# Macaron transformer block: a rearranged first feed-forward stage

## The chip, the cores and the metric

The kernel runs on one core of a Trainium2 chip. The core has five engines with an instruction stream each: TensorE (PE, matrix products), VectorE (DVE, element-wise work and reductions), ScalarE (ACT, activations and copies), GpSimd (POOL, element-wise work) and SyncE (SP, here only DMA issues). Every engine executes its own stream in order; semaphores hold an instruction until its inputs are there. Data lies in an on-chip memory of 128 partitions (SBUF); products go to banks of a second memory, PSUM, from which DVE and ACT read. The metric is the time of one execution on the device in microseconds (us).

## The reference

The input is x, 4 sequences of 1024 rows of 512 numbers. The block is

```python
x = x + 0.5 * ffn(layernorm(x), w_gate_up, w_proj)
x = x + attention(layernorm(x), Wq, bq, Wk, bk, Wv, bv, Wo, bo)
x = x + 0.5 * ffn(layernorm(x), w_gate_up, w_proj)

def ternary_quant(w_fp32, g=64):
    w = w_fp32.astype(bfloat16)
    w_g = w.reshape(-1, g)
    scale = clip(mean(abs(w_g), -1, keepdims=True), 1e-08, None)
    q = clip(round(w_g / scale), -1, 1)
    w_hat = (q * scale).reshape(w.shape)
    return w + (w_hat - w)

def ffn(x, w_gate_up, w_proj):          # w_gate_up: 4096 x 512, w_proj: 512 x 2048
    gate, up = split(x @ ternary_quant(w_gate_up).T, 2)
    h = silu(gate) * up                 # 2048 wide
    h = h * rsqrt(mean(h * h, -1) + eps)
    return h @ ternary_quant(w_proj).T
```

The attention has 32 query heads and 8 key heads of 16 numbers, with a rotary position code. All products work in float32 precision; in the feed-forward each activation is cut into a rounded high part and the low rest, and both are multiplied with the weight.

## The kernel before

The rows are worked in blocks of 512 (two per sequence). The kernel runs one long chain of stages. The first stage, class `First`, does the feed-forward for the two blocks of sequence 0 and at the same time prepares all feed-forward weights, because they arrive as float32 and must be quantized and transposed. Later stages (`FeedForward`, label "0" to "4") do the feed-forward of the other blocks with the prepared weights, and attention stages lie between. What follows the first stage is not touched by the change.

The hidden width of 2048 is cut into 16 weight groups hc of 128. A group has three parts of 128 x 512 numbers: part 0 gate, part 1 up, part 2 the projection. What a group goes through, with the lines of the kernel before:

- `load` (L415): three DMAs on SP bring the parts as float32 into a tile `w` of 128 x 1536, of which there is one.
- `cast` (L429): ACT rounds them to bfloat16 (`wb`, three buffers).
- `double` (L439): ACT makes twice the absolute value (`twice`, two buffers).
- `scales` (L447): DVE reduces absolute values over 64 columns (L455), makes the scale (L457); `widen` (L462) then lets ACT spread each scale over its 64 columns (`wide`, one buffer).
- `signs` (L470): DVE compares `twice` with `wide` for a mask (L482), takes the sign bit of `wb` (L484) and ORs it with the scale (L485) into `wq` (one buffer).
- `quantize` (L489): DVE subtracts, adds and multiplies with the mask (L494 to L496), as the reference rounds.
- `transpose` (L498): PE transposes each part (L503). ACT copies parts 0 and 1 to SBUF as `guT` (L511) and part 2 as `w_pT` (L505), which stays for the whole kernel. For the later stages POOL casts each `guT` to bfloat16 (`g16`, L513), and SP stores it to DRAM in `d_guT` (L514).

For block k (0 or 1) and group hc the products run thus:

- `product` (L542): for part 0 or 1, four 128-wide chunks of the input, each with the high part `xT` and the low part `xL`: eight matmuls into one PSUM bank with the tag "gu" (L546). After part 0, ACT takes the Silu into `sg` (L555). `start` does both parts.
- `finish` (L563): DVE multiplies Silu(gate) with up: h (L575). Block 1's h are all kept.
- `halves` (L578): ACT rounds h to `high` (L584); then DVE or POOL subtracts for `low` (L585). `tally` (L589): the square of h is added to a running sum `acc` on POOL (L603); for block 0 POOL also makes the square (the function passed in at L662).
- `project` (L237): eight matmuls with `w_pT` (L245) add to four output banks "po". There are four "gu" and four "po" banks, and block 1 can be projected only after block 0's outputs have left theirs.
- `factors` and `end` (L267, L280): PE sums `acc` over the partitions (L258), DVE and POOL make the inverse root, and DVE adds the scaled output to x (L288, four times).

`begin_groups` (L609) is the lead: it loads x, normalizes block 0 (`normal_scales` L100, `normalize` L174, with `turned` L124 for the transposes, ACT's copy to `xT` L131 and DVE's subtraction for `xL` L133), and brings group 0 through its parts. `group(i)`, for i from 0 to 17, is the steady part. In the kernel before block 1 lags block 0 by two groups: group i projects block 0's group i-2, transposes group i, does `start(1, i-2)` and later `start(0, i)`, and on the way quantizes group i+1, reduces the scales of group i+2 and casts group i+3. Block 1's rows are normalized in groups 0 and 1. In the groups 5 to 15 attention weights are loaded, transposed and stored on the side (`attention_weights` L518), and x tiles of the next sequence are loaded. `projection` (L386) follows: it splits block 1's kept h and projects them.

The order is written by hand: within `manual_schedule` each engine's stream takes its instructions in the order of the program. Two such parts that follow one another may be interleaved (the trace has the next stage's weight copies, L94, among the last groups). The order of one group on DVE and ACT is set by these lines:

```python
                steps = self.scales(i + 2)
                self.start(1, i - 2)
                self.signs(i + 1)
...
            self.cast(i + 3)
            self.load(i + 4)
            self.double(i + 2)
            for widen in steps:
                widen()
            if i >= 2:
                self.finish(1, i - 2)
            if 2 <= i < HC:
                self.start(0, i)
            if i >= 2:
                self.quantize(i + 1)
```

Of the kernel before, what the change touches and what calls it, by code (L numbers as in the profile page):

```python
# [37 lines left out]
def tile_macaron_block(  # L38
# [58 lines left out]
    def inverse_root(dst, src, n):  # L97
        nc.gpsimd.tensor_tensor(dst, src, mhalf[:, :n], ALU.pow)

    def normal_scales(tiles, label):  # L100

        n = len(tiles)
        mv = small.tile([P, n, 2], F32, tag="mv", name=f"mv_{label}")
        for i, t in enumerate(tiles):
            st = small.tile([P, 6], F32, tag="st", name=f"st_{label}_{i}")
            nc.vector.bn_stats(st, t)
            nc.vector.bn_aggr(mv[:, i, :], st)
        var = small.tile([P, n], F32, tag="var", name=f"var_{label}")
        nc.vector.tensor_scalar(var, mv[:, :, 1], LN_EPS, None, ALU.add)
        rstd = small.tile([P, n], F32, tag="rstd", name=f"rstd_{label}")  # L110
        inverse_root(rstd, var, n)
        return mv, rstd
# [243 lines left out]
    class First(FeedForward):  # L356
# [7 lines left out]
        def groups(self):  # L364

            self.kept = tc.tile_pool(name="kept", bufs=1)
            self.banks = tc.tile_pool(name="fp0a", bufs=4, space=PSUM)
            self.keep, self.ps = self.kept.__enter__(), self.banks.__enter__()
            self.w, self.wb, self.wide, self.twice, self.q = {}, {}, {}, {}, {}
            self.sg, self.made, self.units, self.parts = {}, {}, {}, {}  # L370
            self.turns, self.turning = [], []

            for n in range(4):
                self.pos.setdefault(0, []).append(
                    self.ps.tile([P, D], F32, tag="po", name=f"po_0a_0_{n}")
                )
            with tc.tile_pool(name="f0a", bufs=1) as wp, tc.tile_pool(name="wstage", bufs=1) as stage:
                self.wp, self.stage = wp, stage
                self.ident16 = stage.tile([P, P], BF16, tag="ident16", name="ident16")
                nc.vector.tensor_copy(self.ident16, ident)  # L380
                with tc.manual_schedule():
                    self.begin_groups()
                    for i in range(HC + 2):
                        self.group(i)

        def projection(self):  # L386
# [25 lines left out]

        ALL = ((0, 12),)

        def load(self, hc):  # L415
            if hc >= HC:
                return
            w = self.stage.tile([P, 12, P], F32, tag="w", name=f"w_{hc}")
            r = slice(hc * P, (hc + 1) * P)
            ru = slice(H + hc * P, H + (hc + 1) * P)  # L420
            nc.sync.dma_start(w[:, 0:4, :], w_gate_up[r, :].rearrange("p (c k) -> p c k", k=P))
            nc.sync.dma_start(w[:, 4:8, :], w_gate_up[ru, :].rearrange("p (c k) -> p c k", k=P))
            nc.sync.dma_start(w[:, 8:12, :], w_proj[:, r].rearrange("(c p) k -> p c k", p=P))
            self.w[hc] = w

        def sixteen(self, name, hc, bufs=1):
            return self.stage.tile([P, 12 * P], BF16, tag=name, name=f"{name}_{hc}", bufs=bufs)

        def cast(self, hc, some=ALL):  # L429
            if hc < HC:  # L430
                if hc not in self.wb:
                    self.wb[hc] = self.sixteen("wb", hc, 3)
                for a, z in some:
                    nc.scalar.copy(
                        self.wb[hc][:, a * P : z * P],
                        self.w[hc][:, a:z, :].rearrange("p c k -> p (c k)"),
                    )

        def double(self, hc, some=ALL):  # L439
            if hc < HC:  # L440
# [57 lines left out]
        def transpose(self, hc, part):  # L498
# [5 lines left out]
            if part == 2:  # L504
                nc.scalar.copy(w_pT[hc].rearrange("p (c k) -> p c k", k=P), pt)  # L505
                return
            name = f"guT_{hc}_{part}"
            w = (widened.tile if part else self.stage.tile)(
                [P, DC, P], F32R, tag="guT", name=name, bufs=3
            )  # L510
            nc.scalar.copy(w, pt)  # L511
            w16 = narrow_tile(f"g16_{hc}_{part}")
            nc.gpsimd.tensor_copy(w16, w.bitcast(F32))  # L513
            nc.sync.dma_start(d_guT[hc, part], w16.rearrange("p c k -> p (c k)"))  # L514
            for k in range(2):
                self.weights.setdefault((k, hc), []).append(w)

        def attention_weights(self, n):  # L518

# [21 lines left out]

        def product(self, k, hc, part):  # L542
            pg = self.ps.tile([P, 512], F32, tag="gu", name=f"gu_0a_{k}_{hc}_{part}")
            for c in range(DC):
                for low, xp in enumerate(self.inputs[k]):
                    nc.tensor.matmul(  # L546
                        pg,
                        lhsT=self.weights[k, hc][part][:, c, :],
# [2 lines left out]
                        stop=(c == DC - 1 and low == 1),  # L551
                    )
            if part == 0:
                sg = self.sg[k, hc] = self.wp.tile([P, 512], F32, tag="sg", name=f"sg_0a_{k}_{hc}")
                nc.scalar.activation(sg, pg, AF.Silu)  # L555
            else:
                self.made[k, hc] = pg
# [50 lines left out]

        def begin_groups(self):  # L609

            thirds = [((a, a + 4),) for a in (0, 4, 8)]
            for i in range(4):
                load_x(0, i)
            self.load(0)
            for i in range(4, NT):
                load_x(0, i)
            for third in thirds:
                self.cast(0, third)
            self.load(1)
            self.double(0, thirds[0])  # L620
            scales = normal_scales(self.tiles(0), "0a_0")
            for widen in self.scales(0, thirds[0]):
                widen()
            turns = list(self.normalize(0, range(4), self.wp, self.ps, "gu", 4, scales))
            self.signs(0, thirds[0])
            self.quantize(0, thirds[0])
            for turn in turns:
                turn()
            steps = self.scales(0, thirds[1])
            self.double(0, thirds[1])  # L630
            steps[0]()
            self.transpose(0, 0)
            self.product(0, 0, 0)
            self.signs(0, thirds[1])
            self.quantize(0, thirds[1])
            steps = self.scales(0, thirds[2])
            self.double(0, thirds[2])
            steps[0]()
            self.transpose(0, 1)
            self.cast(1)  # L640
            self.load(2)
            self.double(1)
            self.product(0, 0, 1)
            self.signs(0, thirds[2])
            self.quantize(0, thirds[2])
            self.transpose(0, 2)
            self.cast(2)
            self.load(3)
            for widen in self.scales(1):
                widen()  # L650

        def group(self, i):
            self.finish(0, i - 1)
            if 2 <= i:
                for some in ([0, 1], [2, 3]):
                    self.project(0, i - 2, self.parts[0, i - 2][0], some)
            if i == HC + 1:
                self.end(0, self.factors(0))
            if 1 <= i <= HC:
                self.halves(0, i - 1, nc.gpsimd)  # L660
                self.parts[0, i - 1][1]()
                self.tally(0, i - 1, lambda dst, h: nc.gpsimd.tensor_tensor(dst, h, h, ALU.mult))  # L662
            if 1 <= i < HC:
                for part in range(3):
                    self.transpose(i, part)
            if i < 2:
                if i > 0:
                    self.start(0, i)
                some = [2 * i, 2 * i + 1]
                self.signs(i + 1)  # L670
                self.quantize(i + 1)
                steps = self.scales(i + 2)
                scales = normal_scales(self.tiles(1, some), f"0a_1_{i}")
                rows = list(self.normalize(1, some, self.wp, self.ps, "gu", 4, scales))
                for turn in self.turning:
                    turn()
                self.turning = rows
            else:
                for turn in self.turning:
                    turn()  # L680
                self.turning = []
                steps = self.scales(i + 2)
                self.start(1, i - 2)
                self.signs(i + 1)
            if 5 <= i < 15:
                self.turns.append(self.attention_weights(i - 5))
            self.cast(i + 3)
            self.load(i + 4)
            self.double(i + 2)
            for widen in steps:  # L690
                widen()
            if i >= 2:
                self.finish(1, i - 2)
            if 2 <= i < HC:
                self.start(0, i)
            if i >= 2:
                self.quantize(i + 1)
            if 6 <= i < 16:
                self.turns.pop(0)()
            if 2 <= i < 2 + NT:  # L700
                load_x(1, i - 2)
# [771 lines left out]
```

## Time and profile before

| | before |
|---|---|
| median of 3 runs | 3166.78 us (3166.61 to 3167.30) |
| profiled execution | 3165.26 us, span 3163.5 us |
| PE busy | 3089.3 us (98%), mean granted clock 0.991 |
| DVE / ACT / POOL busy | 2177.3 / 1757.6 / 915.2 us |
| first block-0 product (L546) | 17.94 us |
| 0 to 60 us, PE busy | 25 of 60 us, clock 0.91, 0.50, 0.67 in thirds |
| transposes of the steady groups (L503) | at 104.65, 115.27, 125.91, 136.53 us |
| 100 to 180 us, of each 20: PE, DVE, ACT, POOL | 19.3 to 20.0, 19.7, 13.6 to 15.2, 11.6 to 11.9 |
| first matmul of block 1's projection (L245) | 220.48 us |

Times of single instructions are microseconds from the start of the span. A row in order of time has the start, the length, the engine, the line, the operation, output and inputs with their shapes, how many equal ones were merged, and in brackets how long the engine had been idle before and what released it. A row of a stretch has its bounds, its length and the busy time of PE, PE's weight loads, DVE, ACT and POOL (instructions in brackets), the clock granted to PE, the share of DMA and GB/s. Matmuls are pipelined, so each is listed longer than the distance to the next, and ends on PE are modelled.

### The profile page before, as it was taken

The page shows a single profiled execution, that of the slowest core. Times are in us where ns is not written, and L with a number is a line of the kernel's source. Part 1 is how long each engine was busy: PE and PEld are TensorE (multiplying, and loading weights), DVE is VectorE, ACT ScalarE, POOL GpSimd, SP SyncE. Part 2 cuts the span into 40 slices and gives each one's busy share as a digit, 9 for nine tenths or more (in the row PEclk, how much of TensorE's full clock was granted, in tenths as well). Part 3 has the DMA queues.
Part 4 walks back from the last instruction along what each step waited for, and adds up shares of the span by engine and source line. Part 5 has one row for each costly group of instructions (what it writes and reads, how often), then busy time and mean ns, then how long its engine had stood idle before and what let it go on. Part 6 is the DMA issues. An engine that isn't in the chain of part 4 may idle for free. (4 is left out here: it accounts for less than half of the span.)

```text
span 3163.5 us, 46228 instructions
## 1 busy us (share of the span) xinstructions
PE 3089.3 (98%) x16896; PEld 1953.4 (62%) x16896; DVE 2177.3 (69%) x3656; ACT 1757.6 (56%) x2346; POOL 915.2 (29%) x865
## 2 busy tenths in 40 slices
PE   5999999999999999999999999999999999999999
PEld 4777777733358777533387777333587776333787
DVE  7977666588846665788666665888556666887343
ACT  5752333389953333699913333899523335999343
POOL 2564333300034343200053333000243432000344
PEclk7999999999999999999999999999999999999999
DMA  3443322224334133143242222243341231342111
GB/s 110 156 136 97 92 62 80 60 87 107 115 89 127 55 94 109 48 125 95 89 121 85 88 81 62 76 111 117 88 131 56 77 97 62 94 126 66 40 60 41
DMA packets 231267, 285.52 MB, mean 90 GB/s; under 512 B 30048, under 2 KB 176736, under 8 KB 231040
## 3 DMA queue, kind: packets, MB, share of 16 engines
q1 hardware_dynamic: 224448, 272.32, 29.1%
q0 software_dynamic: 6592, 10.24, 1.4%
q8 instruction: 134, 2.20, 0.3%
q14 instruction: 93, 0.76, 0.1%
HBM read 215.35 MB, written 66.45 MB: 89 GB/s over the span
## 5 line engine op out<-in xcount | busy, mean ns | idle before, releaser
L1171 DVE TENSOR_REDUCE pm<-sm 128x1 f32<-128x512 f32 x2048 | 1281.8, 684 | 207.8 <-PE sm L1162 202.0
L1302 ACT ACTIVATE e<-s 128x1024 f32<-128x1024 f32 x1024 | 990.7, 1023 | 124.9 <-PE s L1293 121.7
L205 PE MATMUL gu<-xT,guT 128*128 128x512 f32 x1792 | 706.9, 394 | 4.3 <-DVE ql L1088 2.8
L205 PE MATMUL gu<-xL,guT 128*128 128x512 f32 x1792 | 700.8, 391 | 0.7 <-DVE xL L133 0.7
L1309 PE MATMUL o<-e,vs 128*32 128x512 f32 x4096 | 548.2, 604 | 0.0
L1162 PE MATMUL sm<-p_m,p_m 64*128 64x512 f32 x2048 | 491.9, 411 | 5.9 <-DVE h L217 5.9
L1293 PEld LDWEIGHTS s<-p_s,p_s 64*128 64x128 f32 x2048 | 193.8, 183 | 483.7 <-ACT e L1302 466.0
L1293 PE MATMUL s<-p_s,p_s 64*128 64x512 f32 x2048 | 467.7, 451 | 8.8 <-ACT e L1302 8.7
L225 POOL TENSOR_TENSOR sq<-h 128x512 f32<-128x512 f32 x210 | 218.7, 1042 | 713.9 <-DVE h L217 713.9
L217 DVE TENSOR_TENSOR h<-sg,gu 128x512 f32<-128x512 f32 x224 | 153.8, 686 | 375.4 <-PE gu L205 361.6
L215 ACT ACTIVATE sg<-gu 128x512 f32<-128x512 f32 x224 | 134.2, 599 | 479.5 <-PE gu L205 479.5
L205 PEld LDWEIGHTS gu<-xT,guT 128*128 128x128 f32 x1792 | 337.8, 188 | 78.8 <-ACT guT L94 3.2
L205 PEld LDWEIGHTS gu<-xL,guT 128*128 128x128 f32 x1792 | 337.8, 188 | 71.9 <-DVE xL L133 1.3
L245 PE MATMUL po<-w_pT,high 128*128 128x512 f32 x896 | 374.2, 418 | 0.9 <-DVE x L288 0.9
L245 PE MATMUL po<-w_pT,low 128*128 128x512 f32 x896 | 355.0, 396 | 0.0
L231 ACT CAST high<-h 128x512 fp32r<-128x512 f32 x224 | 139.0, 621 | 327.0 <-DVE h L217 320.6
L1162 PEld LDWEIGHTS sm<-p_m,p_m 64*128 64x128 f32 x2048 | 229.6, 185 | 83.3 <-DVE h L217 50.2
L229 POOL TENSOR_TENSOR acc<-acc,sq 128x512 f32<-128x512 f32 x205 | 275.9, 1346 | 16.1
L94 ACT CAST guT<-g 128x512 fp32r<-128x512 bf16 x448 | 274.9, 614 | 7.9 <-ACT guT L94 5.5
L245 PEld LDWEIGHTS po<-w_pT,high 128*128 128x128 f32 x896 | 168.2, 188 | 94.3 <-issue 56.4
L1309 PEld LDWEIGHTS o<-e,vs 128*32 128x32 f32 x4096 | 81.1, 108 | 183.3 <-issue 156.0
L233 DVE TENSOR_TENSOR low<-h,high 128x512 fp32r<-128x512 f32 x224 | 169.1, 755 | 35.4 <-ACT high L231 35.4
(159 smaller groups left out, 2869.3 us busy)
## 6 DMA issues: line engine op xcount, KB each, us to landing
g<-d_guT SPq DMA_DIRECT2D x448, 128.0 KB
p_m<-d_q SPq DMA_DIRECT2D x56, 512.0 KB
p_s<-d_q SPq DMA_DIRECT2D x56, 512.0 KB
d_o<-oT SPq DMA_DIRECT2D x64, 256.0 KB
p_m<-d_km SPq DMA_DIRECT2D x56, 256.0 KB
p_s<-d_ks SPq DMA_DIRECT2D x56, 256.0 KB
x<-in_L_attn_x_dram SPq DMA_DIRECT2D x32, 256.0 KB
w<-in_L_ffn_w_gate_up_dram SPq DMA_DIRECT2D x32, 256.0 KB
```

Of the source, the lines that this page charges most:

```text
L94: nc.scalar.copy(w, t)
L205: nc.tensor.matmul(pg, lhsT=self.weights[k, hc][part][:, c, :], rhs=xp[:, c, :], start=(c == 0 and low == 0), stop=(c == DC - 1 and low == 1),
L217: nc.vector.tensor_tensor(h, sg, gu[1], ALU.mult)
L225: nc.gpsimd.tensor_tensor(sq, h, h, ALU.mult)
L229: nc.gpsimd.tensor_tensor(acc, acc, sq, ALU.add)
L233: return (high, low), lambda: nc.vector.tensor_tensor(low, h, high.bitcast(F32), ALU.subtract)
L245: nc.tensor.matmul(self.pos[k][i], lhsT=h[:, i * P : (i + 1) * P], rhs=w_pT[hc], start=(hc == 0 and n == 0), stop=(hc == HC - 1 and n == 1),)
L1162: nc.tensor.matmul(s, lhsT=q[j // 2][at, i * P : (i + 1) * P], rhs=k[at, half * 512 : (half + 1) * 512], start=True, stop=True,)
L1171: nc.vector.tensor_reduce(pm[:, i, j, half : half + 1], s, AX.X, ALU.max)
L1293: nc.tensor.matmul(s[:, e, :], lhsT=lhsT[at], rhs=rhs[at, queries], start=(kc == 0 and n == 0), stop=(n == len(terms) - 1), skip_group_che ...
L1302: return w, lambda: nc.scalar.activation(w, s, AF.Exp, scale=1.0 / HD**0.5)
L1309: nc.tensor.matmul(o[j * SLOT : (j + 1) * SLOT, :], lhsT=vs[:, kc, g, :], rhs=es[j // 2][:, j % 2, :], start=(kc == 0), stop=(kc == NT - 1),)
```

## The change

Block 1 no longer lags. In each group both blocks' products of that weight group are made, block 0's first. The rows of block 1 are normalized in the lead, and the lead brings groups 0 and 1 through both blocks' products; `group` then runs from i = 2.

Inside a group the order is new: transposes first, then h of block 1's last group, `halves` and `tally` of block 0's last group, the projection of block 0's group i-2, signs of group i+1, cast and double of group i+2, block 0's products, quantize of group i+1, the narrow copies, scales and widening of group i+2, h of block 0, block 1's products.

Weights are loaded in thirds into four buffers of 128 x 512; each cast of a third issues the load of the third four further on. `wb` and the part-0 `guT` have two buffers instead of three, and `sg` two instead of one. The narrow copies (`g16`) are made by ACT in `narrow_ones`, a step of its own, instead of by POOL in `transpose`. A product takes its four high matmuls first and then the four low ones. An activation on a single column at the start makes ACT load the table with Silu early. The end of the loop changes with it: block 0's last projection and sums now come after all products.

```diff
-    def normal_scales(tiles, label):
+    def normal_scales(tiles, label, between=lambda i: None):
...
             nc.vector.bn_aggr(mv[:, i, :], st)
+            between(i)
...
-                    for i in range(HC + 2):
+                    for i in range(2, HC + 2):
                         self.group(i)
...
+        def load(self, upto):
+            while self.loaded < min(upto, 3 * HC):
+                hc, part = divmod(self.loaded, 3)
+                w = self.stage.tile([P, DC, P], F32, tag="w", name=f"w_{hc}_{part}", bufs=4)
...
+                nc.sync.dma_start(w, src)
+                self.w[hc, part] = w
+                self.loaded += 1
...
+        def cast(self, hc, parts=range(3)):
             if hc < HC:
                 if hc not in self.wb:
-                    self.wb[hc] = self.sixteen("wb", hc, 3)
+                    self.wb[hc] = self.sixteen("wb", hc, 2)
+                for part in parts:
                     nc.scalar.copy(
+                        self.wb[hc][:, part * 512 : (part + 1) * 512],
+                        self.w.pop((hc, part)).rearrange("p c k -> p (c k)"),
                     )
+                    self.load(3 * hc + part + 5)
...
             nc.scalar.copy(w, pt)
-            w16 = narrow_tile(f"g16_{hc}_{part}")
-            nc.gpsimd.tensor_copy(w16, w.bitcast(F32))
-            nc.sync.dma_start(d_guT[hc, part], w16.rearrange("p c k -> p (c k)"))
+            self.wide_ones.append((hc, part, w))
...
+        def narrow_ones(self):
+            for hc, part, w in self.wide_ones:
+                w16 = narrow_tile(f"g16_{hc}_{part}")
+                nc.scalar.copy(w16, w.bitcast(F32))
+                nc.sync.dma_start(d_guT[hc, part], w16.rearrange("p c k -> p (c k)"))
+            self.wide_ones = []
...
-            for c in range(DC):
-                for low, xp in enumerate(self.inputs[k]):
+            for low, xp in enumerate(self.inputs[k]):
+                for c in range(DC):
...
         def begin_groups(self):
...
+            warm = self.stage.tile([P, 1], F32, tag="warm", name="warm")
+            nc.scalar.activation(warm, ones, AF.Silu)
+            load_x(0, 0)
+            load_x(0, 1)
+            self.load(1)
+            load_x(0, 2)
+            load_x(0, 3)
+            self.load(3)
             for i in range(4, NT):
                 load_x(0, i)
+            self.load(4)
+            normal = normal_scales(self.tiles(0), "0a_0", first_third)
+            self.double(0, b)
+            scales(0, b)
+            turns = list(self.normalize(0, range(4), self.wp, self.ps, "gu", 4, normal))
+            quantized(0, a)
             for turn in turns:
                 turn()
             self.transpose(0, 0)
             self.product(0, 0, 0)
+            quantized(0, b)
             self.transpose(0, 1)
+            self.cast(0, [2])
             self.product(0, 0, 1)
+            normal = normal_scales(self.tiles(1), "0a_1")
+            self.double(0, c)
+            scales(0, c)
+            turns = list(self.normalize(1, range(4), self.wp, self.ps, "gu", 4, normal))
+            self.finish(0, 0)
+            for turn in turns:
+                turn()
+            self.cast(1, [0])
+            self.double(1, a)
+            self.product(1, 0, 0)
+            self.product(1, 0, 1)
+            quantized(0, c)
+            scales(1, a)
             self.transpose(0, 2)
+            self.cast(1, [1, 2])
+            quantized(1, a)
+            rest = ((4, 12),)
+            self.double(1, rest)
+            scales(1, rest)
+            self.transpose(1, 0)
+            self.finish(1, 0)
+            self.product(0, 1, 0)
+            quantized(1, rest)
+            self.transpose(1, 1)
+            self.narrow_ones()
             self.cast(2)
+            self.double(2)
+            self.product(1, 1, 0)
+            self.transpose(1, 2)
+            scales(2, self.ALL)
+            self.product(0, 1, 1)
+            self.finish(0, 1)
+            self.halves_of(0)
+            self.product(1, 1, 1)
+            quantized(2, self.ALL)
+            self.cast(3)
+            self.double(3)
+            scales(3, self.ALL)
 
         def group(self, i):
+            if i < HC:
+                for part in range(3):
+                    self.transpose(i, part)
+            self.finish(1, i - 1)
+            if i <= HC:
+                self.halves_of(i - 1)
+            for some in ([0, 1], [2, 3]):
+                self.project(0, i - 2, self.parts[0, i - 2][0], some)
             if i == HC + 1:
                 self.end(0, self.factors(0))
+                return
+            self.signs(i + 1)
+            if i < HC:
+                self.cast(i + 2)
+                self.double(i + 2)
+                self.start(0, i)
+            self.quantize(i + 1)
+            self.narrow_ones()
+            steps = self.scales(i + 2)
+            for widen in steps:
+                widen()
+            if i < HC:
+                self.finish(0, i)
+                self.start(1, i)
             if 5 <= i < 15:
                 self.turns.append(self.attention_weights(i - 5))
             if 6 <= i < 16:
                 self.turns.pop(0)()
             if 2 <= i < 2 + NT:
                 load_x(1, i - 2)
```

Here `first_third` casts, doubles and scales the first third of group 0 after the second x tile's statistics and casts the second third; `quantized` is signs and quantize together; `scales` in the lead also widens; `halves_of(hc)` is `halves`, `low` and `tally` for block 0, on ACT and POOL as before.

## The prediction

> **What bounds the kernel now.** I read the page first, then the busy time by stretches of 20 us, then the instructions in order of time.
>
> ```profile
> PE 3089.3 (98%) x16896; PEld 1953.4 (62%) x16896; DVE 2177.3 (69%) x3656; ACT 1757.6 (56%) x2346; POOL 915.2 (29%) x865
> ```
>
> TensorE (PE) is the bound of the whole span, so the change can only win where PE idles or runs slow, and loses wherever it makes PE wait. The changed stage covers the first 250 us:
>
> ```profile
> 20.00:40.00 20.00, 7.87 (x33) 5.26 (x31) 12.50 (x20) 11.25 (x11) 0.62 (x1) 0.50 0.36 112
> 40.00:60.00 20.00, 11.18 (x48) 8.69 (x48) 17.16 (x27) 10.13 (x13) 7.53 (x7) 0.67 0.22 66
> 140.00:160.00 20.00, 20.00 (x108) 16.01 (x107) 19.75 (x19) 15.15 (x20) 11.60 (x10) 1.00 0.52 154
> ```
>
> Columns after the length are PE, weight loads, VectorE (DVE), ScalarE (ACT), GpSimd (POOL), the granted clock, DMA. Up to 60 us PE is mostly idle and half-clocked: the lead. From then on DVE is as full as PE (19.75 of 20). One weight group of that stretch, instruction by instruction:
>
> ```profile
> 83.85 1.75 DVE L455 TENSOR_REDUCE wmean<-wb 128x24 f32<-128x1536 bf16 x1
> 84.67 1.30 POOL L585 TENSOR_TENSOR low_0a<-h_0a,high_0a 128x512 fp32r<-128x512 f32 x1 [4.12 <-ACT high_0a L584]
> 85.63 0.36 DVE L457 TENSOR_SCALAR wscale<-wmean 128x24 bf16<-128x24 f32 x1
> 85.91 0.95 DVE L482 TENSOR_TENSOR twice<-twice,wide 128x1536 bf16<-128x1536 bf16 x1
> 85.91 1.84 POOL L662 TENSOR_TENSOR sq_0a<-h_0a 128x512 f32<-128x512 f32 x1
> 86.78 1.39 DVE L484 TENSOR_SCALAR wq<-wb 128x1536 uint16<-128x1536 uint16 x1
> 87.83 1.49 POOL L603 TENSOR_TENSOR acc_0a<-acc_0a,sq_0a 128x512 f32<-128x512 f32 x1
> 88.20 1.93 DVE L485 TENSOR_TENSOR wq<-wq,wide 128x1536 uint16<-128x1536 uint16 x1
> 89.27 1.89 POOL L513 CAST g<-guT 128x512 bf16<-128x512 f32 x2
> 90.06 0.67 DVE L575 TENSOR_TENSOR h_0a<-sg_0a,gu_0a 128x512 f32<-128x512 f32 x1
> 90.66 1.31 DVE L494 TENSOR_TENSOR wq<-wq,wb 128x1536 bf16<-128x1536 bf16 x1
> ```
>
> The round closes every 10.62 us (reduces start at 105.11, 115.73, 126.36). The same DVE operations with POOL idle, in the lead, and the scale's way on to ACT:
>
> ```profile
> 33.69 0.55 DVE L484 TENSOR_SCALAR wq<-wb 128x1536 uint16<-128x1536 uint16 x1
> 34.27 0.96 DVE L485 TENSOR_TENSOR wq<-wq,wide 128x1536 uint16<-128x1536 uint16 x1
> ...
> 39.90 0.18 DVE L457 TENSOR_SCALAR wscale<-wmean 128x24 bf16<-128x24 f32 x1
> ...
> 40.17 1.47 ACT L462 COPY wide<-wscale 128x1536 bf16<-128x1536 bf16 x1 [1.58 <-DVE wscale L457]
> ```
>
> So a POOL operation beside DVE costs DVE time: the mask (L484) 1.39 against 0.55 beside the square, the OR (L485) 1.93 against 0.96 beside the running sum, the subtraction 1.31 against 0.96 beside a cast. The reduce ran 1.75 beside `low`, as it does alone: no loss. The operations take turns; a POOL operation that waits runs as soon as the DVE operation in progress ends.
>
> **A new circle in each group.** Write h(k,i) for block k's product of gate and up in weight group i. In the old order, the scale of group i+2 was reduced before the signs, and ACT had its widening (L462) done before both products' Silu that mattered. In the new order DVE does h(1,i-1), signs(i+1), quantize(i+1), reduce(i+2) and scale, h(0,i), h(1,i). ACT does, in its order, Silu(0,i), two narrow copies, widen(i+2), Silu(1,i). Widen(i+2) waits for the scale, Silu(1,i) stands behind it on ACT, and h(1,i), the head of DVE's next round, needs Silu(1,i). The circle is h(1,i-1) to h(1,i), and nothing in it overlaps. From start to start with POOL idle: h 0.60, compare 0.87, mask 0.58, OR 1.00, subtract, add and multiply 0.99+0.99+0.87 (35.27 to 38.12), reduce 1.78, scale to widen 0.27, widen to the next ACT instruction 1.36 (69.84 to 71.20), Silu and hand-over 0.63. Sum 9.94 us.
>
> Then POOL. `low`, square and running sum of h(0,i-1) start after ACT's copies of the three transposed weights and `high`: with the circle at 0 when Silu(1,i-1) ends, copies at 0, 0.5, 1.0 and `high` 1.5 to 2.1; with an attention weight's copy before them, 2.63. The OR runs from 2.05 to 3.05, so `low` waits for its end and then holds off the subtraction, the square the addition, the sum the multiplication. Prices: 0.95 for `low` (an OR of 1.91 beside it at 45.69), 0.84 for the square, 0.87 for the sum (88.20 row, start to start 1.86 against 1.00). Together 2.66: the circle is 12.60 us. Bounds from the same rows: 9.94 if all three fall beside the reduce, 12.60 if none does. I take the upper end, because the margin of 0.4 us holds for both kinds of group and one POOL operation follows the other at once.
>
> The Trainium skill ("SBUF — State Buffer", on the pair of ports that VectorE and GpSimd share) says the pair is locked for the whole instruction and the later one blocks, that a VectorE instruction with two SBUF inputs competes so with a GpSimd one that reads SBUF, and that a reduce never does. The rows agree on who blocks and on the reduce, but the loss is shorter than the POOL operation (0.95 beside one of 1.28). By the rule's full length the circle would be 13.5 us, and the forecast some 10 us longer.
>
> PE's own work in a group: 32 products at 0.228 = 7.3, 8 projections 1.86, 12 transposes 0.65, sometimes 4 more 0.36: 9.8 to 10.2. So PE waits 2.4 us or more each group, where it waited nearly nothing (one gap of 0.53 between 75 and 215 us). At 320.7 PE idled 2.80 us and the clock fell to 0.50; if that happened every group, PE would need up to 2.6 more, 12.6, still no longer than the circle. The skill ("TensorE: Matmul & The Clock Gate", Part 1) puts the fall at an idle window of about 3.4 us; the row at 2.80 is shorter and decides, and by the rule nothing would be added.
>
> **The lead.** It is laid out by the rows' durations, engine by engine. Loads in thirds put the first third after two x tiles: cast at 5.8 (7.59 before). DVE takes stats and first scale to 10.2, normalized rows to 12.2, first quantization (2.45) to 14.7, four xL to 17.2; product (0,0) starts at 15.9 (17.94 before), now high halves first. Silu's table load (1.28 at 17.91) moves to the start. Second third 19.7, block 1's stats and rows to 26.1, h(0,0), xL to 29.3, third third and first third of group 1 to 36.0, the rest of group 1 (reduce 1.2, quantize 3.9) to 42.45. Then ACT: transposed copy, four narrow copies (2.2), cast(2) 1.7 to 47.7; reduce 49.45; ACT ends widen(2) at 51.6; quantize(2) 5.33 plus 1.8 for two collisions, 58.75; scales(3) before h(1,1): 60.75. First circle 13.45, since widen(3) ends only at 62.15: h(1,2) at 74.2. Four of 32 double products are then counted ahead of PE's 62.7, where the old kernel had two at 62.31: a gain of 7.3, less one projection and one set of transposes (2.5). The waits in this layout are hand-overs of 0.03 to 0.3; I allow 4 us either way.
>
> **The tail.** Before, block 1's last product stood between the sums and block 1's projection:
>
> ```profile
> 215.93 0.95 PE L258 MATMUL pq_0a<-ones,acc_0a 128*128 128x1 f32 x8
> 218.42 2.73 DVE L288 SCALAR_TENSOR_TENSOR x<-po_0a,half_0a,x 128x512 f32<-128x512 f32 x4
> 220.48 0.40 PE L245 MATMUL po_0a<-w_pT,high_0a 128*128 128x512 f32 x1
> ```
>
> Now nothing does: PE waits for the factors and for DVE to free the first output bank, 2.5 (215.93 to 218.42) plus 0.7. High and `low` of group 15 also stand behind ACT's last attention copy: 0.7 before the last projection, 0.6 for the sum. Bounds 2.5 and 7; I take 4.5 in all against 0 before.
>
> **The rest costs nothing, while its cover stands.** Two narrow copies move from POOL to ACT (0.6 each), cast in thirds is 1.9 instead of 1.47: ACT's group is 9.7 of 12.6, it idles before widen. Were ACT the bound, 9.7 would be under PE's 10.2. On SP the two d_guT writes now follow ACT's copies; behind them are an attention load and store, an x load and the next thirds, which are issued four thirds ahead (some 13 us; a load issued at 32.28 was cast at 35.74). Two buffers for wb and guT instead of three: both are released in the group before. The casts off POOL give back the 0.35 of the subtraction, contained in the circle.
>
> **Sum.** h(1,2) 74.2 + 11 circles of 12.60 (groups 3 to 13) = 212.8. Groups 14 and 15 have no widen and run at PE's pace: 0.25+1.86+7.3+0.36 = 9.8, then 0.5 for a bank and 10.2: 233.3. Projections 2 x 1.86 and waits 1.3: 238.3 for the sums; +3.2: 241.5 for block 1's first projection, 220.48 before: +21. All that follows is unchanged and hangs on PE. Profiled execution 3165.26 + 21 = 3186.3; its median stands 1.5 higher (3166.78): 3187.8.
>
> **Rivals.**
> 1. One or two POOL operations miss (`low` comes after the OR has ended and the sum falls beside the reduce). Circle 10.9 to 11.7, 3169 to 3178. For it: `high` is late by 0.4 us. Against: only ACT's four copies stand before it.
> 2. Faster: POOL's operations stay clear of the circle, as `low` did beside the reduce at 84.67. Then it is 9.94, under PE's 10.2, and PE sets the pace: 11 x 10.2 instead of 138.6, 26 less: 3161, and 3157 if the lead is 4 better. It decides once the loss is below some 0.75 per group, less than one collision (circle under 10.7). Against: ACT, PE and DVE begin the round together, which puts POOL early in it.
> 3. Worse: each collision blocks for the whole POOL operation (1.28+1.04+1.27 instead of 2.66), or the clock falls each group and PE's wait adds to the circle: 0.9 to 1.5 more per group, 3198 to 3206.
>
> **How the numbers follow.** Forecast 0.50 (own range 3180 to 3195), rival 1 0.20, rival 2 0.17, rival 3 0.13. A measurement of this kernel tells 0.2% (6.3 us) from no change. Faster: rival 2 with a good lead, 0.11. Same: its rest and the low edge of rival 1, 0.10. Slower 0.79. The range 3165 to 3204 leaves out rival 2 and the top of rival 3.
>
> **What would show it.** Right: ACT's L462 waiting 3 to 4 us a group for wscale, DVE's h for ACT's Silu, POOL interleaved with subtract, add, multiply at 1.3 to 1.9 each, transposes 12.6 apart, block 1's projection at about 241. Wrong: transposes 10.2 apart, or DVE's three operations at 0.96. A lead that ends well before 56 would also break it.

## The result, and the profile after

| | before | after |
|---|---|---|
| median | 3167.04 us (3166.61 to 3168.71) | 3189.89 us (3188.74 to 3191.82) |
| profiled execution | 3165.26 us, span 3163.5 | 3189.67 us, span 3187.7 |
| first block-0 product | 17.94 us | 15.92 us |
| 0 to 60 us, PE busy | 24.95 us | 30.90 us |
| 75 to 215 us, PE busy | 139.28 us | 122.38 us |
| block 1's first projection | 220.48 us | 242.55 us |

The changed kernel takes 1.0073 of the time [1.0058, 1.0088]: 22.85 us more. The forecast was 3187.8 us with a range of 3165 to 3204. The first projection of block 1, which closes the changed stage, moved by 22.07 us, so nearly all of the loss lies in that stage.

The busy times over the whole span have hardly moved; only the stretches of the stage tell the two kernels apart. These are the page's first part and the stretches that answer to those shown before:

```profile
PE 3096.7 (97%) x16896; PEld 1958.9 (61%) x16896; DVE 2183.1 (68%) x3663; ACT 1774.9 (56%) x2410; POOL 892.5 (28%) x832
```

```profile
20.00:40.00 20.00, 13.19 (x53) 9.42 (x54) 17.84 (x40) 10.65 (x18) 1.01 (x1) 0.76 0.18 54
...
140.00:160.00 20.00, 18.30 (x83) 14.60 (x82) 17.94 (x16) 12.94 (x19) 8.94 (x6) 0.91 0.52 157
```

In the lead PE does more than before: 30.90 of the first 60 us against 24.95, most of the gain in the second stretch (13.19 of 20 against 7.87). That part of the change does what it was made for. From 140 to 160 us, where PE had been busy for the full 20.00 at clock 1.00, it now has 18.30 at 0.91, and no other engine is full either: DVE fell from 19.75 to 17.94. So every engine waits for something. The waits between 75 and 215 us name no transfer, only other engines; the chief ones are (waiting engine and line, releaser, total, times, longest):

```profile
POOL low_0a L598 <- ACT high_0a L597: 88.8, 12, 8.2
ACT wide L467 <- DVE wscale L462: 38.6, 11, 4.2
...
DVE h_0a L588 <- ACT sg_0a L568: 15.6, 11, 1.4
PE pw L508 <- ACT sg_0a L568: 9.0, 9, 1.0
PE pw L508 <- DVE h_0a L588: 8.6, 16, 1.4
```

POOL has the least work and waits longest. Two of the other waits occur once in each of the 11 groups: ACT's widening waits for DVE's scale (3.5 us on average), and DVE's h waits for ACT's Silu (1.4 us). PE's 17.6 us of waiting hang on the same Silu and h. DVE and ACT wait for each other in a ring, the circle of the prediction. Here is one turn of it in order of time: the rows of DVE and POOL, and the two of ACT that close the ring. Left out are DVE's compare, mask and OR after the first row, block 0's h before the widening, ACT's other rows, and all rows of PE and SP:

```profile
135.88 0.69 DVE L588 TENSOR_TENSOR h_0a<-sg_0a,gu_0a 128x512 f32<-128x512 f32 x1 [1.42 <-ACT sg_0a L568]
...
138.38 1.68 POOL L598 TENSOR_TENSOR low_0a<-h_0a,high_0a 128x512 fp32r<-128x512 f32 x1 [7.23 <-ACT high_0a L597]
138.94 1.94 DVE L499 TENSOR_TENSOR wq<-wq,wb 128x1536 bf16<-128x1536 bf16 x1
140.02 1.76 POOL L709 TENSOR_TENSOR sq_0a<-h_0a 128x512 f32<-128x512 f32 x1
140.91 1.68 DVE L500 TENSOR_TENSOR wq<-wq,wb 128x1536 bf16<-128x1536 bf16 x1
141.85 1.89 POOL L616 TENSOR_TENSOR acc_0a<-acc_0a,sq_0a 128x512 f32<-128x512 f32 x1
142.62 1.93 DVE L501 TENSOR_TENSOR wq<-wq,twice 128x1536 bf16<-128x1536 bf16 x1
144.48 1.74 DVE L460 TENSOR_REDUCE wmean<-wb 128x24 f32<-128x1536 bf16 x1
146.26 0.18 DVE L462 TENSOR_SCALAR wscale<-wmean 128x24 bf16<-128x24 f32 x1
...
146.47 1.47 ACT L467 COPY wide<-wscale 128x1536 bf16<-128x1536 bf16 x1 [3.57 <-DVE wscale L462]
147.84 0.59 ACT L568 ACTIVATE sg_0a<-gu_0a 128x512 f32<-128x512 f32 x1
148.47 0.69 DVE L588 TENSOR_TENSOR h_0a<-sg_0a,gu_0a 128x512 f32<-128x512 f32 x1 [1.42 <-ACT sg_0a L568]
```

From h at 135.88 to h at 148.47 there is no hole: DVE works from 135.88 to 146.4, ACT widens and takes the Silu to 148.43, and DVE begins again. This turn is 12.59 us. Inside it the subtraction (L499), addition (L500) and multiplication (L501) took 1.94, 1.68 and 1.93 instead of 0.96 each, with one POOL operation beside each.

The seven turns with an attention weight on the side look like this and take 12.58 to 12.59 us. The four turns without one, at the start, take 12.71 to 12.72 us, and there POOL comes one DVE operation earlier: `low` starts at 87.18, just ahead of the OR (L490), and the multiplication is spared. DVE's stream:

```profile
87.23 2.06 DVE L490 TENSOR_TENSOR wq<-wq,wide 128x1536 uint16<-128x1536 uint16 x1
89.32 1.68 DVE L499 TENSOR_TENSOR wq<-wq,wb 128x1536 bf16<-128x1536 bf16 x1
91.03 1.94 DVE L500 TENSOR_TENSOR wq<-wq,wb 128x1536 bf16<-128x1536 bf16 x1
93.00 0.96 DVE L501 TENSOR_TENSOR wq<-wq,twice 128x1536 bf16<-128x1536 bf16 x1
```

The eleven turns run from 72.45 to 211.38, 138.93 us.

### The profile page after: what moved, and what is told of

Read it like the earlier page. It is cut to its first block, busy times and chain, and to the rows that moved or that the text cites. A ratio compares the mean times of both kernels' runs of the same rounds, so it can differ in the third digit from the quotient of the medians.

```text
span 3187.7 us, 46200 instructions
## 1 busy us (share of the span) xinstructions
PE 3096.7 (97%) x16896; PEld 1958.9 (61%) x16896; DVE 2183.1 (68%) x3663; ACT 1774.9 (56%) x2410; POOL 892.5 (28%) x832
```

## The experiments

One measure serves beside the total time: the start of block 1's first projection, 220.48 us before and 242.55 after. What follows it is the same program everywhere, but its length varied by up to 3 us between the profiles (from an equal point in the next stage to the end of the span: 2906.1 before, 2908.9 after, 2905.6 to 2908.9 in the others). So a difference of up to 3 us in total time is not put down to an edit unless the projection, or block 1's own sums some 30 us behind it, moves as well.

| run | time us | ratio to before | projection us | turn or round us |
|---|---|---|---|---|
| after | 3189.89 | 1.0073 [1.0058, 1.0088] | 242.55 | 12.58 to 12.71 |
| e1 widening behind | 3167.46 | 1.0003 [0.9994, 1.0013] | 222.85 | 10.51 to 11.49 |
| e2 square on ACT | 3177.68 | 1.0035 [1.0021, 1.0050] | 232.74 | 11.86 to 11.99 |
| e3 no squares | 3167.68 | 1.0003 [0.9993, 1.0012] | 221.51 | 10.89 to 11.02 |
| e4 casts on POOL | 3190.75 | 1.0077 [1.0062, 1.0092] | 246.51 | 12.58 to 13.0 |
| e5 scales first | 3160.44 | 0.9982 [0.9974, 0.9991] | 215.53 | 9.96 to 10.53 |
| e6 e5, tail shifted by two | 3159.10 | 0.9974 [0.9964, 0.9985] | 215.65 | as e5 |
| e7 before, copies on ACT | 3164.90 | 0.9995 [0.9986, 1.0004] | 218.35 | 10.25 |
| e8 e5, old table load and order | 3159.60 | 0.9981 [0.9972, 0.9990] | 215.38 | as e5 |
| e9 e5, last product shifted | 3157.43 | 0.9972 [0.9961, 0.9982] | 214.59 | as e5 |

Where a turn has two values, one is that of the groups with an attention weight on the side and the other that of the groups without: with one the turn is the shorter in after, e1, e2, e3 and e4, and the longer in e5.

### e1: open the ring at ACT, keep the collisions

```diff
             steps = self.scales(i + 2)
-            for widen in steps:
-                widen()
             if i < HC:
                 self.finish(0, i)
                 self.start(1, i)
+            for widen in steps:
+                widen()
```

> The changed kernel with one move: in each group the widening of group i+2's scale stands behind block 1's Silu on ScalarE instead of ahead of it. No instruction is added or taken away. The theory (a circle h - signs - quantize - reduce - widen - Silu - h closes every 12.59 us) says that the circle now closes on VectorE alone: 8.4 us of its own instructions, 2.67 us of turns with GpSimd, 0.4 us in which the comparison waits for the widening, so about 11.4 us a group where all three GpSimd operations still fall beside the quantization, and about 10.6 in the groups with an attention weight, where they come later and one falls beside the reduce. 11 groups: 12 to 19 us shorter, 3171 to 3178. The rival that the extra time comes from GpSimd's turns alone, or from the narrow copies on ScalarE, says no change, 3188 to 3191.

3167.46 us, 22.4 less than after, with nothing changed but the place of one ACT instruction in its queue. The Silu now runs before the widening, and both h follow the scale without a wait. DVE's stream from the addition to the next compare:

```profile
132.91 1.93 DVE L500 TENSOR_TENSOR wq<-wq,wb 128x1536 bf16<-128x1536 bf16 x1
134.88 1.68 DVE L501 TENSOR_TENSOR wq<-wq,twice 128x1536 bf16<-128x1536 bf16 x1
...
138.26 0.18 DVE L462 TENSOR_SCALAR wscale<-wmean 128x24 bf16<-128x24 f32 x1
138.37 1.33 DVE L588 TENSOR_TENSOR h_0a<-sg_0a,gu_0a 128x512 f32<-128x512 f32 x2
139.97 0.96 DVE L487 TENSOR_TENSOR twice<-twice,wide 128x1536 bf16<-128x1536 bf16 x1 [0.27 <-ACT wide L467]
```

Both h are in the row at 138.37, and DVE waits only 0.27. Collisions are still there: in this round the addition took 1.93 and the multiplication 1.68, and in groups without an attention weight the subtraction took 1.93 as well. The round is DVE's own work and that short wait, 10.51 or 11.49. The order on ACT was the ring's closing link. The total is below the expected 3171 to 3178, although the rounds are as long as expected. The projection came 19.7 us earlier; the other 2.7 of the 22.4 us are within what the part behind it varies by.

### e2 and e3: take POOL operations away, keep the ring

```diff
-            self.tally(0, hc, lambda dst, h: nc.gpsimd.tensor_tensor(dst, h, h, ALU.mult))
+            self.tally(0, hc, nc.scalar.square)
```

> The changed kernel, with block 0's squares made by ScalarE instead of GpSimd; the same result. The theory says that one of three collisions goes (0.72 us measured beside the addition) and that ScalarE has the time, since it idles 3.57 us ahead of each widening: circle about 11.8 us, 11 groups, 8 to 9 us shorter: 3181. If the circle does not pass through VectorE's quantization, nothing changes; if ScalarE is short of time, it gets longer.

```diff
-            self.tally(0, hc, lambda dst, h: nc.gpsimd.tensor_tensor(dst, h, h, ALU.mult))
+            if hc == 0:
+                self.tally(0, hc, lambda dst, h: nc.gpsimd.tensor_tensor(dst, h, h, ALU.mult))
```

> The changed kernel without the squares and running sums of block 0 after its first weight group, so the scaling of block 0's first feed-forward is left out in part. Two of three collisions go (0.72 and 0.97 us): the theory says a circle of 10.9 us, 18 to 20 us shorter, 3170 to 3172, with VectorE's addition and multiplication at 0.96 us each. If the lock is not what makes these long, they stay at 1.7 to 1.9 and the time stays at 3188 to 3191.

With the square on ACT, DVE's three operations are 1.94, 1.94 and 0.96. DVE's stream of e2:

```profile
134.69 1.94 DVE L499 TENSOR_TENSOR wq<-wq,wb 128x1536 bf16<-128x1536 bf16 x1
136.66 1.94 DVE L500 TENSOR_TENSOR wq<-wq,wb 128x1536 bf16<-128x1536 bf16 x1
138.63 0.96 DVE L501 TENSOR_TENSOR wq<-wq,twice 128x1536 bf16<-128x1536 bf16 x1
```

There are two collisions, and the turn is 0.72 shorter (12.58 to 11.86), as the sum of the losses is (0.98 + 0.98 = 1.96 against 0.98 + 0.72 + 0.97 = 2.67). e3 leaves out block 0's squares and running sums after the first weight group, so it does not compute the block's scaling in full; of POOL's three operations only `low` is left, beside the subtraction. DVE's stream of e3:

```profile
140.22 1.93 DVE L499 TENSOR_TENSOR wq<-wq,wb 128x1536 bf16<-128x1536 bf16 x1
142.19 0.96 DVE L500 TENSOR_TENSOR wq<-wq,wb 128x1536 bf16<-128x1536 bf16 x1
143.18 0.96 DVE L501 TENSOR_TENSOR wq<-wq,twice 128x1536 bf16<-128x1536 bf16 x1
```

The turn is 10.89, 1.69 less than 12.58, and 0.72 + 0.97 is 1.69. So the losses on the DVE operations enter the turn in full, one by one. ACT still idles before the widening (3.57 us in after, 2.33 in e2), so its own work isn't the limit, not even with a square more. The times are 3 us below what was expected; 1.0 of it is a wait for the running sum before the sums matmul, which is gone in both. The rest is not explained by the stage and lies within what the part behind it varies by: e2's projection comes 9.8 us earlier than after's, its time is 12.2 us less.

### e4 and e7: the copies' engine by itself

```diff
                 w16 = narrow_tile(f"g16_{hc}_{part}")
-                nc.scalar.copy(w16, w.bitcast(F32))
+                nc.gpsimd.tensor_copy(w16, w.bitcast(F32))
```

> The changed kernel with the narrow copies back on GpSimd, at the same place in the order: one part of the change undone. The theory says that they come after the running sum, beside the reduce, where nothing is held up, and that ScalarE's 1.2 us were idle time: circle 12.6 us, 3186 to 3193. The rival that ScalarE's added work is what costs says some 10 us shorter or more; the hope behind the part (VectorE is freed of two collisions) says longer by 0.3 us or more a group, 3193 or more.

e7 is the opposite edit in the kernel before: only its two narrow copies a group go from POOL to ACT.

> The kernel before, with one part of the change alone: the narrow copies are made by ScalarE, right behind the copy of each transposed part. In the old order the casts on GpSimd hold up VectorE's subtraction by 0.35 us a group and the round closes on VectorE at 10.62 us. The theory says that the subtraction falls to 0.96 us and the round to TensorE's pace, 10.3 to 10.5 us: 9 rounds, 1 to 3 us shorter, 3164 to 3166. If ScalarE's 1.1 us more a group delay the Silu and with it a bank or h, longer, 3169 or more.

In the new order the engine of the copies matters little: 3190.75 against 3189.89 us. In the groups with an attention weight the turn keeps 12.58, since POOL makes its two casts (1.89) beside DVE's reduce, which takes 1.74 as ever. In the four groups without one the casts begin beside the multiplication, which takes 1.25 instead of 0.96, and the turn is 13.0. The projection comes 4.0 us later than in after: 0.9 in the lead, 1.1 in the four turns of 13.0, 2.0 behind the last turn. So putting the copies on ACT did not cost the 22 us; it saved some 4 at that point, which the total time shows only in part. In the old order the copies were worth little: DVE's subtraction falls from 1.31 to 0.95 and the round from 10.62 to 10.25, but PE's transposes are 10.33 apart. That PE takes over as the limit is read from these two numbers; no run tries it. The projection comes 2.1 us earlier; the time, 0.9995 [0.9986, 1.0004], can't be told from before.

### e5: open the ring at DVE, and with it the collisions

```diff
-            self.quantize(i + 1)
             self.narrow_ones()
             steps = self.scales(i + 2)
             for widen in steps:
                 widen()
+            self.quantize(i + 1)
```

> The changed kernel with the reduce, the scale and the widening of group i+2 (and the narrow copies with them) moved ahead of the quantization of group i+1. Nothing is added or taken away. The theory says that two things go at once: the widening is done before block 1's Silu is due, so the circle is open, and low, square and sum fall mostly beside the reduce, which is not held up. VectorE then needs 9.7 us a group, less than TensorE's 9.9 to 10.3, so TensorE sets the pace: 11 groups, 22 to 26 us shorter, 3164 to 3168. The rival that the lead or the tail lost the time says 3185 or more.

3160.44 us: 29.5 less than after and 0.9982 [0.9974, 0.9991] of before. DVE reduces the next scale before the three long operations, so ACT's widening runs while DVE quantizes. DVE's and POOL's streams of e5, and a stretch:

```profile
146.75 1.75 DVE L460 TENSOR_REDUCE wmean<-wb 128x24 f32<-128x1536 bf16 x1 [1.50 <-ACT wb L438]
...
148.87 0.94 DVE L499 TENSOR_TENSOR wq<-wq,wb 128x1536 bf16<-128x1536 bf16 x1
...
150.84 0.96 DVE L501 TENSOR_TENSOR wq<-wq,twice 128x1536 bf16<-128x1536 bf16 x1
```

```profile
145.24 1.30 POOL L598 TENSOR_TENSOR low_0a<-h_0a,high_0a 128x512 fp32r<-128x512 f32 x1 [6.85 <-ACT high_0a L597]
```

```profile
140.00:160.00 20.00, 20.00 (x109) 16.45 (x108) 16.02 (x20) 16.92 (x28) 7.20 (x6) 1.00 0.55 161
```

POOL's three operations (`low` in the row, then square and sum to 148.92) now lie in DVE's wait for the cast (1.50) and beside the reduce, at their own length of 1.30, 1.04 and 1.30, and DVE's three are at 0.94 to 0.96. Only the small scale operation still meets the sum: it takes 0.41 instead of 0.18 here and 0.99 in a group without an attention weight, and DVE has that time to spare. PE is busy for 20.00 of 20 at clock 1.00 and sets the round: 9.96, or 10.53 with an attention weight. The time is 4 us below the 3164 to 3168 expected. This answers where the gain went: with the ring open and the collisions gone the change is worth 4.95 us at the projection (220.48 to 215.53), and the closed ring with the collisions in it costs 27.0 (215.53 to 242.55).

### e8: two small parts undone

e5 without the early load of Silu's table, and with high and low product matmuls by turns as in the kernel before:

```diff
-            for low, xp in enumerate(self.inputs[k]):
-                for c in range(DC):
+            for c in range(DC):
+                for low, xp in enumerate(self.inputs[k]):
...
-            nc.scalar.activation(warm, ones, AF.Silu)
+            nc.vector.tensor_copy(warm, ones)
```

> The kernel with the scales first, without two small parts of the lead: no early Silu (so the table with Silu is loaded when the first Silu comes) and the old order inside a product (high and low by turns). By the rows of the lead the critical thread runs through VectorE and ScalarE's casts and not through the first product, so the theory says within 1.5 us of the kernel with the scales first, 3159 to 3162. If the products are the critical thread of the lead, 2 to 3 us longer.

3159.60 us, projection at 215.38: no difference to e5 (215.53). The table load stands again at 16.65 us for 1.28 us and is hidden there.

### e6 and e9: the tail

Both are additions to e5 and put block 1's products of the last weight group (15) behind block 0's sums. e6 also puts those of group 14 off, behind block 0's products of group 15; e9 does not. The edit of e9, less that of e5:

```diff
             if i == HC + 1:
                 self.end(0, self.factors(0))
+                self.start(1, HC - 1)
+                self.finish(1, HC - 1)
                 return
...
                 self.finish(0, i)
-                self.start(1, i)
+                if i < HC - 1:
+                    self.start(1, i)
```

> As the kernel with the scales first, and block 1's products of the last two groups put off: those of group 14 stand behind block 0's products of group 15, those of group 15 behind block 0's sums, so that TensorE has work while low, sum, factors and the outputs of block 0 are awaited. In the changed kernel TensorE waits there for 0.58, 1.00 and 3.16 us. The theory says 4 to 5 us less than with the scales first alone, 3159 to 3163, which is less than the kernel before (3167). If the tail's waits only move into the projection of block 1, no difference to the kernel with the scales first.

> The kernel with the scales first, and only block 1's products of group 15 put behind block 0's sums. With two groups put off, TensorE lost 1.66 us waiting for the quantization of group 15, because group 14 had become short; that wait should go. Of the tail's 0.58 + 1.00 + 3.16 us the 3.16 should be covered by 3.65 us of products: 3 us less than the scales first alone, 3156 to 3159. If the wait returns in block 1's projection (for high or low), 3160.

e5 still has after's tail: PE waits 0.58, 1.00 and 3.16 us. In e9 the last wait is filled with the 16 product matmuls of one block's group; PE's stream after the sums is unbroken to the projection:

```profile
208.32 1.05 PE L259 MATMUL pq_0a<-ones,acc_0a 128*128 128x1 f32 x8 [0.89 <-POOL acc_0a L616]
209.24 1.41 PE L559 MATMUL gu_0a<-xT_0a,guT 128*128 128x512 f32 x4
...
214.59 0.40 PE L246 MATMUL po_0a<-w_pT,high_0a 128*128 128x512 f32 x1
```

e9 takes 3157.43 us, 0.9972 [0.9961, 0.9982] of before: less than before and after, and 3.0 less than e5. At the projection it is only 0.94 ahead of e5, but the wait has a second price that lies behind this mark. After its 3.16 us, e5 starts the projection with products 0.43 apart, where e9 has 0.23, and the clock granted over the next 7.5 us is 0.74 against 1.00:

```profile
216.10 0.63 PE L246 MATMUL po_0a<-w_pT,low_0a 128*128 128x512 f32 x1
216.53 0.63 PE L246 MATMUL po_0a<-w_pT,high_0a 128*128 128x512 f32 x1
```

(These are e5's rows.) Where block 1's own sums begin, e9 is 2.79 ahead (242.68 against 245.47). e6 missed its expected 4 to 5 us: at these sums it is no earlier than e5 (245.81), so the 1.3 us less in its time isn't shown to come from the edit. With products taken from group 14 too, that group is too short for DVE, and PE waits for the last quantization. e6's row:

```profile
194.82 0.98 PE L508 MATMUL pw<-ident,wq 128*128 128x128 bf16 x12 [1.66 <-DVE wq L501]
```

## Why the prediction was right

**The new circle** was the step that decided, and it stood. Its terms were 9.94 us without POOL and three collisions at 0.95, 0.84 and 0.87, together 2.66. In the turns with an attention weight 0.98, 0.72 and 0.97 were measured, together 2.67, and turns of 12.58 to 12.59 against 12.60. The single prices were off by up to 0.12 in both directions, so the agreement to 0.01 is luck. e1 shows that the ring closes through the place of the widening ahead of Silu, e2 and e3 that the collisions add one by one, e5 that both go when the scale comes first. The eleven circles took 138.93 us (forecast 138.6).

One step inside it failed in four of the eleven turns. The margin of 0.4 us, by which `low` was to come during the OR in both kinds of group, holds only with an attention weight: by the prediction's own figures `high` ends at 2.1 without one and the OR begins at 2.05. There `low` came 0.05 us ahead of the OR (87.18 against 87.23), and the collisions fell on the OR, the subtraction and the addition: 1.10, 0.72 and 0.98, together 2.80. The turn grew by 0.13 only, since three POOL operations in a row still met three such DVE operations in a row.

**PE** was to wait 2.4 us or more a group, and the clock perhaps to fall without lengthening the circle. The named waits are less, 17.6 us in eleven groups. In the eight turns at a clock of 1.00 PE idled 1.7 us with an attention weight and 2.2 to 2.4 without: it was busy for 10.3 to 10.9 us of a turn, where 9.8 to 10.2 had been reckoned. In the other three the clock fell to 0.86 or 0.87 and stretched PE's work, and it idled 0.4 to 1.0. The lowest stretch is at 84 us:

```profile
84.00:88.00 4.00, 3.00 (x14) 2.40 (x12) 2.80 (x4) 4.00 (x8) 0.82 (x1) 0.65 0.00 0
```

The turn with this stretch was 12.71, as long as its neighbours at clock 1.00: PE's slack took it, as forecast.

**The lead** was mis-sized by 1.9 us: h(1,1) came at 58.84 instead of 60.75, within the 4 allowed. Most of that was there by group 2's reduce, which began at 46.01 instead of 47.7. The first circle was 13.61 (13.45).

**The tail.** The waits of 0.58 and 1.00 had been put at 0.7 and 0.6. From the sums to the projection it took 4.21 instead of 3.2. The term that failed is the 2.5 up to DVE's first addition, read from a place where the factor `half` took 0.17. Here it fell beside a memset of POOL's for the attention stage that follows, and took 0.90:

```profile
240.65 0.95 POOL L1421 MEMSET even_rows<- 128x1024 f32 x1
240.72 0.90 DVE L278 TENSOR_SCALAR half_0a<-inv_0a 128x4 f32<-128x4 f32 x1 [1.13 <-POOL inv_0a L98]
...
242.55 0.77 PE L246 MATMUL po_0a<-w_pT,high_0a 128*128 128x512 f32 x1 [3.16 <-DVE x L289]
```

(After in order of time, from the memset to the projection; DVE's first addition starts at 241.65, the sums at 238.34.) The projection was forecast at 241.5 and came at 242.55, and errors cancel in that: the lead and first circle were 1.75 shorter than forecast, the eleven circles 0.33 longer, groups 14 and 15 with block 0's last projections 1.46 longer (26.96 instead of 25.5 from h(1,13) to the sums), the tail 1.0 longer. **The rest at no cost** stood: the copies on ACT cost nothing (with POOL making them, e4's projection came 4.0 us later), nor did the table load and the order of the matmuls (e8). That all behind the projection is unchanged holds to within the 3 us by which that part varies.

**The rivals.** Rival 1, one or two collisions missing, did not come about by itself; e2 and e3 brought it about, at turns of 11.9 and 10.9. Its reckoning by the circle alone gave 3169 to 3178 for 10.9 to 11.7; e3 measured 3167.7 at 10.9, e2 3177.7 at 11.9. Rival 2, PE setting the pace, had been put at 3161, and 3157 with a lead 4 us better. e5 made its condition true, but opened the ring as well, and took 3160.4. e9 got to 3157.4, but by the tail, not the lead. Rival 3, each collision as long as the whole POOL operation, fell: the three losses in the turns with an attention weight are each about 0.3 us less than POOL's 1.30, 1.04 and 1.30 in e5, where nothing holds them up. (Its upper price of 1.5 us a group would have made 3204, not 3206.) The Trainium skill ("SBUF — State Buffer", on the shared pair of ports) has the pair locked for the whole instruction; the later operation did block here, yet the rule's full length would have made the turn 3.64 instead of 2.67 longer than 9.94, and the measurement decides.

## What to carry to other kernels

When instructions change places in the streams of in-order engines, follow each one's input and successor once round all engines: a step on ACT that waits for DVE, placed ahead of something that DVE needs next, makes a ring whose parts add up, though no engine is full. Price its members at what they cost beside the neighbours that they will have there, and look for the cheapest cut: here moving one call was worth 29 us (e5). A wait that falls out of a tail is best filled with work that is independent of it, and no more than the group that gives it away can spare.

## What was not expected of the hardware

A DVE operation on 128 x 4 numbers (`half`) took 0.89 to 0.90 us in all seven profiles where a POOL memset, which reads nothing, ran beside it (after, e1 to e5, e8), and 0.17 in all four where POOL stood idle at that moment (before, e6, e7, e9). That the memset held it up is read from the rows' times; it was not tried by itself.

The clock fell to 0.65 over 84 to 88 us, though PE's named waits between 75 and 215 us were at most 1.4 us each. It fell in three of the eleven turns only: ahead of 84 us PE had waited 1.44 and 1.00 us with four transposes between, and it waited as long, with as much between, from 107.8 to 110.6 us, where the clock stayed at 1.00. How the gaps of a turn add up to such a fall stays open.
